# Loading the context in 2 KB pieces, chunk by chunk, beside transposes through DRAM

## The chip, the core and the metric

The kernel runs on one core of one Trainium2 chip. The time is that of the device for one launch, in microseconds (us); lower is better. The engines are TensorE (PE, with its weight loads PEld), VectorE (DVE), ScalarE (ACT), GpSimd (POOL) and SyncE (SP). ScalarE, SyncE and GpSimd also issue DMAs, each on a queue of its own.

## What is computed

One block of a perceiver on 16 items, all in float32: each item has 128 tokens of width 512 and a context of 2048 rows of width 512.

```python
# x: (16, 128, 512), ctx: (16, 2048, 512)
h = layernorm(x)
x = x + softmax(h @ ctx.T) @ ctx                       # cross attention on the context
h = layernorm(x)                                       # 16 heads, latent 64, head size 32
q, k, v = up(h @ Wq_down), up(h @ Wk_down), up(h @ Wv_down)   # half of q and k rotated
x = x + (softmax(causal(q @ k.T / sqrt(32))) @ v) @ Wc
h = layernorm(x)
gates = softmax_of_top2(h[:, 0] @ Wr.T)                # 2 of 8 experts, by the first token
x = x + h + sum_e gates[e] * (h @ A[e].T) @ Bw[e].T
```

## The kernel before

The work of an item `b` is cut into generators, which yield between parts: `score(b)` (first layernorm, scores against the context, softmax without its division), `attend(b)` (probabilities times context, division, residual, second layernorm), `inner(b)` (self attention, third layernorm) and `experts(b)` (gating, two gathered experts, result). A hand-written sequence of `step(kind, b)` calls (lines 985 to 1095) interleaves them, so that in turn `b` of the main loop (line 1050) `inner(b)`, `attend(b + 1)`, `score(b + 2)` and `experts(b - 1)` run together, and the layernorm of item `b + 3` as well. The last two items run in an order that is written out in `CLOSING` (line 48). Matmuls, TensorE transposes and loads keep the order of the program on their engine (`keep_in_program_order`, lines 136 to 145), and so do the instructions marked `pinned`.

The context comes from DRAM twice. `ctxT` is the context turned, laid out by the host for the scores; `load_turned` (line 339) brings it in four chunks of 1 MB, each 128 partitions by 4 by 512 numbers. `ctx` has the rows as they are, for `attend`; `load_ctx` (line 345) brings it in four chunks of 1 MB too. Both sets of tiles live in a pool of four buffers per name, so a chunk can be loaded once the same chunk of the item before has been used: a chunk of `ctxT` after its 16 score products (line 397), a chunk of `ctx` after its quarter of `attend` (line 459). In both loads each partition takes one piece of 8 KB: the host lays `ctxT` out so, and partition `p` takes rows `4p` to `4p + 3` of a chunk of `ctx`. From the main loop on both are issued on ScalarE's queue (`queue = nc.scalar`, line 1049): the four chunks of `ctx` of item `b + 2` after the third score bank is copied, the four of `ctxT` of item `b + 3` after the fourth bank and the copies of `yT` and `vv`. There they stand between the activations of that engine.

Activations are transposed in two steps. VectorE turns 32 by 32 blocks (into `blocks`, or `pX` for the probabilities of the self attention), and the blocks change place by a way through DRAM: `send` (line 224) writes them to a DRAM tile `there`, and `fetch` (line 232) reads them back, in pieces of 512 bytes into `hT` or of 1 KB into `pT`. These DMAs are all on SP's queue, and a fetch waits for its send to land. In each turn the two halves of the probabilities (`p_b_0`, `p_b_1`) and the second layernorm of item `b + 1` (`2_{b+1}`) go this way at the end of the self attention's softmax. TensorE uses `pT` in `y` (`weighted`, line 658) and the `hT` of item `b + 1` in `v` (`project`, line 528), after the score products of item `b + 2`, the expert's `mid` and its second product.

The softmax of `inner` is `weigh` (line 643), in four groups of four heads: mask, maximum, four exponentials on ScalarE, division, and the transposing of blocks. The chosen experts' weights are gathered by GpSimd (`each`, `wb`, lines 803 to 813).

Of the kernel before, what the change touches and what calls it, by code (L numbers as in the profile page):

```python
# [19 lines left out]
P = 128  # L20
B, S, V, D = 16, 128, 2048, 512
# [3 lines left out]
KC = D // P  # L25
VC = V // 512
# [15 lines left out]
MIX = [p % 4 * QD + p // 4 for p in range(P)]  # L42
# [47 lines left out]
def perceiver_block(ctx: ExitStack, tc: tile.TileContext, io: dict, out: bass.AP):  # L90
# [53 lines left out]
    def load(*args, queue=nc.sync):  # L144
        tc.keep_in_program_order(queue.dma_start(*args))

    queue = nc.sync
# [76 lines left out]
    def send(name):  # L224
        if name in ways:
            blocks, dst = ways[name]
            each = blocks.shape[2] * QD
            there = dram.tile([P, 4 * each], F32, tag=f"there_{each}", name=f"there_{name}")
            load(there, blocks.rearrange("p q n j -> p (q n j)"))
            ways[name] = there, dst  # L230

    def fetch(name):
        if name in ways:
            there, dst = ways.pop(name)
            load(
                dst.rearrange("p a n j -> p a (n j)"),
                there.rearrange("(a i) (q e) -> (i q) a e", a=4, q=4),
            )
# [94 lines left out]
    def load_x(b):  # L333
        xs[b] = p3.tile([P, D], F32, tag="x", name=f"x_{b}")
        load(xs[b], io["x"][b])
# [3 lines left out]
    def load_turned(b, vs=range(VC)):  # L339
        for v in vs:  # L340
            t = p4.tile([P, KC, 512], F32, tag="ctxT", name=f"ctxT_{b}_{v}")
            load(t, io["ctxT"][b, v], queue=queue)
            turned_cts.setdefault(b, []).append(t)

    def load_ctx(b, vs=range(VC)):
        for v in vs:
            t = p4.tile([P, 4, D], F32, tag="ctx", name=f"ctx_{b}_{v}")

            load(
                t, io["ctx"][b, v * 512 : (v + 1) * 512].rearrange("(p j) d -> p j d", j=4),  # L350
                queue=queue,
            )
            cts.setdefault(b, []).append(t)
# [621 lines left out]
    def step(kind, b, n=1):  # L975
        if not 0 <= b < B:
            return
        if (kind, b) not in gens:
            gens[kind, b] = kind(b)
        for _ in range(n):  # L980
            next(gens[kind, b])
# [11 lines left out]

    warm_up(15)
    load_turned(0, [0, 1])
    load_x(1)
    load_turned(0, [2, 3])
    load_ctx(0, [0])
    load_turned(1, [0, 1])
    load_ctx(0, [1])  # L1000
    load_turned(1, [2, 3])
    load_ctx(0, [2, 3])
    load(up, io["up"])
    step(score, 0, 2)
# [41 lines left out]
    step(inner, 0)  # L1046


    queue = nc.scalar
    for b in range(B - 2):  # L1050
        if b + 3 < B:
            load_x(b + 3)
        step(inner, b)
        step(experts, b - 1)
        send(f"3_{b - 1}")
        fetch(f"3_{b - 1}")
        if b:
            send(f"1_{b + 2}")
            fetch(f"1_{b + 2}")
        step(inner, b, 3)  # L1060
        step(score, b + 1, 2)
        step(attend, b + 1)
        step(inner, b)
        step(attend, b + 1)
        step(inner, b, 2)
        step(experts, b - 1)
        step(attend, b + 1)
        step(inner, b)
        step(attend, b + 1)
        step(experts, b - 1)  # L1070
        step(inner, b)
        step(experts, b - 1)
        step(inner, b + 1)
        send(f"p_{b}_0")
        fetch(f"p_{b}_0")
        send(f"p_{b}_1")
        send(f"2_{b + 1}")
        fetch(f"p_{b}_1")
        fetch(f"2_{b + 1}")
        step(score, b + 2, 2)  # L1080
        step(score, b + 3)
        step(score, b + 2)
        load_ctx(b + 2)
        step(score, b + 2)
        step(experts, b - 1)
        step(score, b + 2)
        step(experts, b - 1)
        step(inner, b)
        step(inner, b + 1)
        if b + 3 < B:  # L1090
            load_turned(b + 3)
        step(score, b + 2)
        step(score, b + 3)
        step(inner, b)
        step(score, b + 2)
# [63 lines left out]
```

## Time and profile before

| | us |
|---|---|
| median of 3 runs (810.36 to 811.34) | 810.94 |
| the profiled execution | 810.97 |
| its span | 809.2 |
| TensorE busy | 800.2 |
| VectorE busy | 529.7 |
| ScalarE busy | 260.4 |
| one turn of the main loop | 47.86 |

In the views, a line gives the engine, the line of the program, the operation, the tile written and those read, the shape and the count. `PEq`, `ACTq` and `SPq` are the sequencers of the engines, which issue DMAs. L137, L140, L115 and L145 are the helpers through which all instructions go, so groups are told apart by their tiles. The DMA engines' busy share is a mean over 16 engines; their queues are q10 (ScalarE's), q1 (SP's) and q0 (GpSimd's).

The matmuls of a turn keep the same order from turn to turn, and a turn of 47.86 us can be read from any pair of equal lines, such as the first product of `y` at 441.14 and at 489.00 us.

### The profile page before, as it was taken

What the parts mean: (1) busy time and instruction counts of PE and PEld (TensorE: products, weight loads), DVE (VectorE), ACT (ScalarE), POOL (GpSimd) and SP (SyncE); (2) the same over time, 40 slices, a digit from 0 to 9 for tenths busy, and PEclk for the clock granted to TensorE, in tenths of its full rate; (3) what the DMA queues carried; (4) which work ended last, traced back from release to release, by engine and by line L of the source; (5) the groups of instructions that cost most, each with busy time, mean ns of one, the idle gap of its engine ahead of it and who ended that gap; (6) DMA issues with size and microseconds to landing.
All of it is one profiled execution on the core that took longest, in us unless ns stands there. A gap on an engine that the chain in (4) does not pass through costs nothing.

```text
span 809.2 us, 14363 instructions
## 1 busy us (share of the span) xinstructions
PE 800.2 (99%) x5538; PEld 568.5 (70%) x5538; DVE 529.7 (65%) x1234; ACT 260.4 (32%) x772; POOL 146.6 (18%) x213
## 2 busy tenths in 40 slices
PE   9999999999999999999999999999999999999996
PEld 9946775768677576866758677676867757686653
DVE  2455759386684947658495775938667584856885
ACT  2232324142232423233241232415223241422461
POOL 1001011212121121211112121111212112121204
PEclk9999999999999999999999999999999999999999
DMA  9998394967849497694958859495885949664102
GB/s 375 417 389 321 118 380 171 340 253 251 360 163 381 172 324 292 221 397 142 364 212 292 320 188 399 152 353 222 281 337 181 388 152 340 261 231 173 41 1 79
DMA packets 76868, 211.05 MB, mean 261 GB/s; under 512 B 6400, under 2 KB 42624, under 8 KB 60416
## 3 DMA queue, kind: packets, MB, share of 16 engines
q10 hardware_dynamic: 15696, 113.32, 35.0%
q1 hardware_dynamic: 57168, 84.75, 29.4%
q0 software_dynamic: 3936, 12.07, 4.4%
q8 instruction: 44, 0.72, 0.3%
q14 instruction: 24, 0.20, 0.1%
HBM read 180.23 MB, written 29.88 MB: 260 GB/s over the span
## 4 chain that ended last, share of the span: by engine, by line
PE 97%; DVE 1%; POOL 0%; issue 0%; ACT 0%; POOLq 0%
PE psc L137 28%; PE av L137 28%; PE k L137 7%; PE q L137 7%; PE v L137 7%; PE o L137 6%; PE pss_sc L137 2%; PE y L137 2%; PE ffn L137 2%; PE pss_acc L137 2%; PE mid L137 2%; PE warm L137 1%; PE tr_m L140 0%; PE tr L140 0%; PE spread L137 0%; PE lg L137 0%
## 5 line engine op out<-in xcount | busy, mean ns | idle before, releaser
L137 PE MATMUL psc<-hT,ctxT 128*128 128x128 f32 x2048 | 235.0, 276 | 0.0
L137 PEld LDWEIGHTS psc<-hT,ctxT 128*128 128x128 f32 x2048 | 231.3, 192 | 0.5 <-issue 0.5
L137 PE MATMUL av<-ctx,sc 128*128 128x512 f32 x512 | 227.3, 596 | 0.0
L137 PEld LDWEIGHTS av<-ctx,sc 128*128 128x128 f32 x512 | 94.4, 190 | 110.5 <-issue 107.9
L115 ACT ACTIVATE att<-att,nmx 128x128 f32<-128x128 f32 x256 | 98.8, 388 | 84.9 <-DVE nmx L115 84.9
L115 POOL TENSOR_SCALAR rs<-mv 128x1 f32<-128x1 f32 x47 | 10.6, 225 | 431.0 <-DVE g_at L115 209.5
L115 ACT COPY sc<-psc 128x512 f32<-128x512 f32 x64 | 37.5, 586 | 140.0 <-PE psc L137 140.0
L115 ACT ACTIVATE sc<-sc 128x512 f32<-128x512 f32 x64 | 40.2, 630 | 90.9 <-DVE sc L115 90.4
L137 PE MATMUL k<-hT,w_k 128*128 128x128 f32 x512 | 60.1, 275 | 0.0
L137 PE MATMUL q<-hT,w_q 128*128 128x128 f32 x512 | 60.0, 275 | 0.0
L137 PEld LDWEIGHTS k<-hT,w_k 128*128 128x128 f32 x512 | 58.5, 192 | 1.5 <-issue 0.8
L137 PE MATMUL v<-w_v,hT 128*32 128x512 f32 x520 | 59.0, 593 | 0.0
L137 PEld LDWEIGHTS q<-hT,w_q 128*128 128x128 f32 x512 | 58.5, 192 | 0.0
L137 PE MATMUL o<-w_c,yT 128*128 128x512 f32 x128 | 57.8, 594 | 0.0
L115 DVE TENSOR_TENSOR mx<-psc,mx 128x512 f32<-128x512 f32 x32 | 21.6, 676 | 55.0 <-ACT sc L115 55.0
L115 ACT ACTIVATE kb<-kT,cst 128x512 f32<-128x512 f32 (+1 forms) x34 | 36.2, 1113 | 39.8 <-DVE kT L115 39.8
L115 DVE TENSOR_SCALAR h<-x,mv,rs 128x512 f32<-128x512 f32 x47 | 27.4, 583 | 31.9 <-POOL rs L115 31.9
L115 ACT ACTIVATION_READ_ACCUMULATOR att<-att,nmx 128x1 f32 x256 | 47.9, 187 | 0.0
L115 DVE TENSOR_TENSOR sc<-sc,spread 128x512 f32<-128x512 f32 x64 | 42.6, 671 | 3.3 <-PE spread L137 3.3
L115 DVE TENSOR_TENSOR att<-att,rsm 128x512 f32<-128x512 f32 x64 | 43.4, 678 | 0.8
L115 DVE TENSOR_REDUCE nmx<-att 128x4 f32<-128x512 f32 x64 | 41.8, 671 | 0.1
L137 PEld LDWEIGHTS o<-w_c,yT 128*128 128x128 f32 x128 | 23.9, 196 | 23.8 <-issue 23.0
(139 smaller groups left out, 851.1 us busy)
## 6 DMA issues: line engine op xcount, KB each, us to landing
ctx<-in_ctx_dram ACTq DMA_DIRECT2D x56, 1024.0 KB, 8.4
ctxT<-in_ctxT_dram ACTq DMA_DIRECT2D x52, 1024.0 KB, 10.5
there_p<-pX SPq DMA_DIRECT2D x28, 512.0 KB, 4.0
pT<-there_p SPq DMA_DIRECT2D x28, 512.0 KB, 4.5
ctxT<-in_ctxT_dram SPq DMA_DIRECT2D x12, 1024.0 KB, 8.9
there<-blocks SPq DMA_DIRECT2D x42, 256.0 KB, 3.3
hT<-there SPq DMA_DIRECT2D x42, 256.0 KB, 3.0
ctx<-in_ctx_dram SPq DMA_DIRECT2D x8, 1024.0 KB, 10.5
```

The source lines that it names most:

```text
L115: ins = issue(*args, **kwargs)
L137: tc.keep_in_program_order(nc.tensor.matmul(*args, **kwargs))
```

## The change

A load of a chunk is made of pieces of 2 KB instead of 8 KB. For `ctxT` the host lays the four parts of a chunk one after the other, each 128 partitions by 2 KB; for `ctx` partition `p` takes rows `p`, `p + 128`, `p + 256` and `p + 384` of the chunk. The order of rows in the scores follows from this in the same way.

The loads are no longer issued four at a time. A chunk of `ctx` is issued after the second, third and fourth group of the self attention's exponentials and after the copy of the first score bank; `ctxT` follows chunk by chunk after the second and third bank and with two chunks after the fourth. The order of the matmuls does not change. The loads before the main loop keep their places.

```diff
     def load_turned(b, vs=range(VC)):
         for v in vs:
             t = p4.tile([P, KC, 512], F32, tag="ctxT", name=f"ctxT_{b}_{v}")
-            load(t, io["ctxT"][b, v], queue=queue)
+            load(t, io["ctxT"][b, v].rearrange("c p n -> p c n"), queue=queue)
...
             load(
-                t, io["ctx"][b, v * 512 : (v + 1) * 512].rearrange("(p j) d -> p j d", j=4),
+                t, io["ctx"][b, v * 512 : (v + 1) * 512].rearrange("(j p) d -> p j d", p=P),
                 queue=queue,
             )
...
         step(attend, b + 1)
         step(inner, b, 2)
+        load_ctx(b + 2, [0])
         step(experts, b - 1)
         step(attend, b + 1)
         step(inner, b)
+        load_ctx(b + 2, [1])
         step(attend, b + 1)
         step(experts, b - 1)
         step(inner, b)
+        load_ctx(b + 2, [2])
         step(experts, b - 1)
         step(inner, b + 1)
         send(f"p_{b}_0")
...
         fetch(f"p_{b}_1")
         fetch(f"2_{b + 1}")
-        step(score, b + 2, 2)
+        step(score, b + 2)
+        load_ctx(b + 2, [3])
+        step(score, b + 2)
+        if b + 3 < B:
+            load_turned(b + 3, [0])
         step(score, b + 3)
         step(score, b + 2)
-        load_ctx(b + 2)
+        if b + 3 < B:
+            load_turned(b + 3, [1])
         step(score, b + 2)
         step(experts, b - 1)
         step(score, b + 2)
+        if b + 3 < B:
+            load_turned(b + 3, [2, 3])
         step(experts, b - 1)
         step(inner, b)
         step(inner, b + 1)
-        if b + 3 < B:
-            load_turned(b + 3)
         step(score, b + 2)
...
         "ctxT": laid(
-            p["ctx_1024"].reshape(B, VC, P, 4, KC, P)[..., MIX].transpose(0, 1, 5, 4, 3, 2)
-        ).reshape(B, VC, P, KC, 512),
+            p["ctx_1024"].reshape(B, VC, 512, KC, P)[..., MIX].transpose(0, 1, 3, 4, 2)
+        ),
```

## The prediction

> **What bounds the kernel now.** I read the page's busy times first, then the chain that ended last, then one turn of the loop in order of time, then the DMA landings, and last the DMA share by stretch.
>
> ```profile
> PE 800.2 (99%) x5538; PEld 568.5 (70%) x5538; DVE 529.7 (65%) x1234; ACT 260.4 (32%) x772; POOL 146.6 (18%) x213
> PE 97%; DVE 1%; POOL 0%; issue 0%; ACT 0%; POOLq 0%
> q10 hardware_dynamic: 15696, 113.32, 35.0%
> q1 hardware_dynamic: 57168, 84.75, 29.4%
> q0 software_dynamic: 3936, 12.07, 4.4%
> ```
>
> TensorE is busy for 800.2 of 809.2 us and makes 97% of the chain. The three DMA queues together fill 69% of the 16 engines: DMA is no bound on average, but it is no idle resource either. Of the 9.0 us that TensorE idles, 1.0 lies ahead of the first matmul and nearly all the rest after 760 us, in the closing order, which the change leaves alone. So there is almost nothing to win, and the question is whether TensorE's order, which it keeps, is made to wait.
>
> One turn of the loop takes 47.86 us. The timeline of TensorE around the end of a turn (start, duration, what):
>
> ```profile
> 462.01 10.57 PE L137 MATMUL av<-ctx,sc 128*128 128x512 f32 x24
> 486.26 1.06 PE L137 MATMUL mid<-hT,wa 128*128 128x128 f32 x8
> 489.00 1.08 PE L137 MATMUL y<-pT,vv 128*32 128x128 f32 x32
> 489.89 2.33 PE L137 MATMUL v<-w_v,hT 128*32 128x512 f32 x20
> ```
>
> And the DMA issues on SP's and ScalarE's queues, the last two lines from the turn before:
>
> ```profile
> 470.53 0.32 SPq L145 DMA_DIRECT2D there_p<-pX  x1
> 473.15 0.37 SPq L145 DMA_DIRECT2D pT<-there_p  x1
> 473.61 0.46 SPq L145 DMA_DIRECT2D there_p<-pX  x1
> 477.82 0.32 SPq L145 DMA_DIRECT2D there<-blocks  x1
> 478.89 0.37 SPq L145 DMA_DIRECT2D pT<-there_p  x1
> 480.55 0.37 SPq L145 DMA_DIRECT2D hT<-there  x1
> 435.98 1.96 ACTq L145 DMA_DIRECT2D ctx<-in_ctx_dram  x4
> 445.80 1.90 ACTq L145 DMA_DIRECT2D ctxT<-in_ctxT_dram  x4
> ```
>
> The transposes through DRAM run from 470.5 on. The second pT landed 4.0 us after its issue, at 482.9, and y needs it at 489.0; hT landed 3.8 us after its issue, at 484.35, and v needs it at 489.89. Over the turns from 138 us on, hT lands 3.4 to 5.5 us ahead of v (some 4.8 on average, 2.9 in the first turn) and pT 3.8 to 6.1 us ahead of y. **These few microseconds are all the cover there is.** The context loads stay out of the way now: ctx is issued at 435.98 + 47.86 = 483.8, when the transposes are all but over, and ctxT at 493.7.
>
> How full the DMA engines are there (stretch, engine columns empty, granted clock, DMA share, GB/s):
>
> ```profile
> 472.00:473.00 1.00, 1.00 0.59 238
> 476.00:477.00 1.00, 1.00 1.08 386
> 482.00:483.00 1.00, 1.00 1.06 372
> DMA packets 1027, 2.04 MB, mean 408 GB/s; under 512 B 32, under 2 KB 32, under 8 KB 1027
> DMA packets 294, 2.12 MB, mean 424 GB/s; under 512 B 35, under 2 KB 35, under 8 KB 35
> ```
>
> The shares from 470 to 484 add up to 9.9 us of all 16 engines. The last two lines are 5 us each of saturated loads: 36 to 41 us, the k weight in pieces of 2 KB (line 287), and 54 to 59, ctxT in pieces of 8 KB. They price the smaller piece: 4% less rate, so 2.57 against 2.47 us a megabyte-load, and 1027/16/5 = 12.8 packets per engine and us, 78 ns each.
>
> [...] The trace is compatible with either size of a turn: a there<-blocks of 256 KB issued at 455.98 beside 8 KB ctxT loads took 4.9 us, against 2.2 to 2.7 away from them; its 8 packets per engine behind 8 packets of 0.31 us are 2.5 us, and that is also one whole load. [...]
>
> **The change part by part.**
>
> *Pieces of 2 KB.* The 64 ctxT and 64 ctx loads go from 128 packets to 512. That adds 0.10 us each, 0.8 us of DMA a turn, hidden by the 31% of free DMA time. Only the head is saturated (share 1.0 from 3 to 75 us). The load with the least room there is ctxT chunk 0 of context 1: it lands at 21.2 and TensorE takes it up at about 22.3. Some 6.8 MB precede it, so it comes 0.7 us later: still in time. I take 0; the bounds are 0 and, if the head ran at the 340 GB/s of some stretches of weight loading at 43 to 48 us, +4.
>
> *Eight DMA issues moved on ScalarE's queue.* They cost 0.34 to 0.56 us each (median 0.41), before and after. Three now stand among the 16 exponentials of 0.385 us that run back to back from 464.7 to 471.0: after the 8th, the 12th and the last. Behind the first two wait groups 2 and 3, and behind these VectorE's scaling and transposes to pX. The second there_p would be ready up to 0.8 us later, but it stands in SP's queue behind the first pT, which lands only at 477.4: hidden. Each ctx issue waits for TensorE to be done with its buffer: quarter 0 of av at 460, quarter 1 at 465.5, quarter 2 at 469.0; the issues fall at some 468.1, 470.0 and 471.8, so none waits. The others come just after the copy of a score bank whose matmuls freed the buffer.
>
> *Completion semaphores.* The 19 hardware DMAs of a turn share eight of these in turn, so each issue waits for the eighth before it. ctx chunk 3 (at 477.3) thus waits for chunk 1, and ctxT chunk 0 (480.7) for ctx chunk 2. Behind the second on ScalarE is the copy of score bank 2, due at 483.8. I put chunk 2's landing at 482 to 483: 1 us of cover, cost 0; if it is gone, the running maximum is late, not TensorE's next matmul. SP's present wait for ctx (98.3 us in 13 turns) goes; it ends before VectorE's blocks are ready, so nothing is gained.
>
> *Loads beside transposes.* This decides. From 468.1 to 489.9, 21.8 us, ScalarE's queue now holds ctx 0 to 3 and ctxT 0 and 1: six loads, 15.0 us at 2.5. With the 9.9 us of transposes and gathers that is 24.9 us of work in 21.8: **3.1 us too much**, so ScalarE's queue is backlogged nearly throughout. From the first there_p to hT, SP's queue has per engine 8 + 32 + 8 + 8 + 32 + 32 = 120 packets. If each lets one 2 KB packet pass, 120 x 78 ns = 9.4 us are added; less the 4.8 us of cover, v waits 4.6 us. That is the upper bound for turns by packet. The lower is 0, if the gaps in SP's chain let ScalarE's queue run dry or SP's packets are hardly held up. The excess of 3.1 us would be the wait if hT were served last; a part falls on ctxT chunk 1. I take 2.7 us a turn. The gathers (3.5 us to landing, wa ready at 481.9 for mid at 486.26) get some 4 us later, inside the same wait.
>
> A wait at v shifts the whole next turn, as attend, softmax and loads all follow from it, so it comes again: 13 turns (contexts 0 to 12; the 14th loads no ctxT) x 2.7 = 35 us.
>
> *Sum.* Span 809.2 + 35 = 844.2; with 810.97 - 809.2 = 1.8 around it, 846. The profiled execution's 810.97 stands 0.03 above the median of 810.94, so the same holds for that.
>
> **The rivals.** A is the forecast.
>
> B, no change: the cover holds. Place: hT ahead of v. Price 0, and the head's 0.7 us hidden: 811. It decides as long as less than 4.8 us are added, that is, if fewer than 62 of the 120 packets have to let one pass. For it: DMA has 31% free over the turn, SP's chain has long gaps, and small reads mixed with large ones reached 386 GB/s. Against it: 24.9 us of work in 21.8.
>
> C, much slower: a turn is a whole load, not a 2 KB packet. Then there_p, there, both pT and hT each wait up to 2.5 us; five of these are 12.5, less 4.8 is 7.7; with some gaps 6.5. 13 x 6.5 = 85: 895.
>
> D, faster: the loads' removal from 483 to 505 would have to shorten head or tail. TensorE idles 9.0 us in all, and I find no DMA that releases those waits in the tail: at most 1 us, 810, and below 809.3 only by something I don't see.
>
> E, the head alone stalls (2 KB pieces at 340 GB/s), the turns do not: +4, 815.
>
> **How the numbers follow.** About 0.2% (1.6 us) is what a measurement of this kernel can tell from no change. Chances: A 0.56, with its own range from 1.4 to 4.5 us a turn, 829 to 869; B 0.20; C 0.13; D 0.04; E 0.07. Slower: A, C and E, 0.76; same: B, 0.20; faster: D, 0.04. The range from 809.5 to 869 holds A, B and E and leaves out C and D, 0.17.
>
> **What would show it.** Right: between 130 and 730 us turns of about 50.6 us instead of 47.86; TensorE waiting at v (or y) for hT (or pT); hT at 7 to 9 us to landing in that place and pT at 6 to 7; DMA share near 1.0 from 470 to 500. Wrong: turns still 47.86 long with hT landing ahead of v (B); pT and there_p at 9 us and more (C); TensorE waiting for ctxT before 50 us (E); copies of the score banks late behind ScalarE's DMA issues, with mx the last to come, which I priced at nothing.

## The result and the profile after

| | before | after |
|---|---|---|
| median, us | 810.65 (4 runs, 810.17 to 811.34) | 998.49 (4 runs, 997.6 to 1002.77) |
| span of the profiled execution, us | 809.2 | 996.0 |
| TensorE busy, us | 800.2 | 840.7 |
| TensorE idle, us | 9.0 | 155.3 |
| one turn, us | 47.86 | 61.9 in the median (58.6 to 64.6) |

The ratio is 1.2327 (95% interval 1.2289 to 1.2364). The kernel became 188 us slower where 35 were forecast. In the experiments below, three of the four runs of the kernel with two early chunks, the profiled one among them, were slow ones (860.46 to 869.35, the fourth 847.45), so it has no ratio. From the page of the changed kernel, the busy times, the chain that ended last, and the queues:

```profile
PE 840.7 (84%) x5538; PEld 577.2 (58%) x5538; DVE 536.3 (54%) x1234; ACT 260.7 (26%) x772; POOL 150.8 (15%) x213
...
q10 hardware_dynamic: 57168, 113.32, 32.3%
q1 hardware_dynamic: 64848, 84.75, 23.7%
q0 software_dynamic: 3936, 12.07, 4.1%
...
DMA 39%; PE 30%; DVE 21%; POOL 4%; issue 3%; SPq 2%; ACT 0%; DVEq 0%; ACTq 0%; POOLq 0%
```

The chain was 97% TensorE. Now DMA leads it, although the queues move the same bytes as before and are busy for 60% of a longer span: it is latency, not volume. TensorE's waits (total in us, times, longest):

```profile
PE y L137 <- DMA pT<-there_p: 110.8, 19, 9.2
PE v L137 <- DMA hT<-there: 32.6, 13, 3.3
PE ffn L137 <- ACT mid L115: 2.6, 2, 2.2
```

The difference of the spans, 186.8 us, is 146.3 us more idle time, nearly all in these two waits, and 40.5 us more busy time of the same 5538 matmuls. The group of `v` shows where most of the latter comes from: 821 ns each, against 593 before, 27.1 us in all.

```profile
L137 PE MATMUL v<-w_v,hT 128*32 128x512 f32 x520 | 86.1, 821 | 32.6 <-DMA hT<-there 32.6
```

One turn on SP's queue and on ScalarE's, and TensorE at its end:

```profile
517.68 0.32 SPq L145 DMA_DIRECT2D there_p<-pX  x1
525.23 0.37 SPq L145 DMA_DIRECT2D pT<-there_p  x1
525.69 1.19 SPq L145 DMA_DIRECT2D there_p<-pX  x1
526.93 0.42 SPq L145 DMA_DIRECT2D there<-blocks  x1
538.00 0.37 SPq L145 DMA_DIRECT2D pT<-there_p  x1
539.29 0.37 SPq L145 DMA_DIRECT2D hT<-there  x1
```

```profile
512.86 0.38 ACTq L145 DMA_DIRECT2D ctx<-in_ctx_dram  x1
514.45 0.37 ACTq L145 DMA_DIRECT2D ctx<-in_ctx_dram  x1
515.95 0.37 ACTq L145 DMA_DIRECT2D ctx<-in_ctx_dram  x1
...
523.41 0.37 ACTq L145 DMA_DIRECT2D ctx<-in_ctx_dram  x1
...
527.07 0.37 ACTq L145 DMA_DIRECT2D ctxT<-in_ctxT_dram  x1
```

```profile
536.02 0.64 PE L137 MATMUL y<-pT,vv 128*32 128x128 f32 x16 [0.18 <-DMA pT<-there_p]
544.90 1.08 PE L137 MATMUL y<-pT,vv 128*32 128x128 f32 x16 [8.24 <-DMA pT<-there_p]
549.24 4.92 PE L137 MATMUL v<-w_v,hT 128*32 128x512 f32 x32 [3.26 <-DMA hT<-there]
```

A fetch is issued as soon as its send has landed (in the kernel before, the last update of the first send's semaphore stands at 473.09 us and its fetch at 473.15). From issue to issue the first send takes 7.55 us (2.62 before), the second 12.31 (5.28). hT then takes 9.95 us to `v` (3.8 to its landing before) and is issued 1.29 us behind the second fetch (1.66 before). The four differences, 4.9 + 7.0 + 6.15 - 0.4, make 17.7 us, of which the cover takes 5.5 (484.35 to 489.89 in the turn before). So `v` starts 12.2 us later after the first send than before; with the slower products this turn is 13.5 us longer.

What the queues move tells how. From 518 to 519 us, just after the send was issued (packets, MB, share of 16 engines):

```profile
DMA packets 158, 0.32 MB, mean 324 GB/s; under 512 B 0, under 2 KB 0, under 8 KB 158
...
q10 hardware_dynamic: 158, 0.32, 98.0%
```

SP's queue, q1, has no line: not one packet of the send has moved. q1's first packets come at 521.9, 4.2 us after the issue; before, 0.8 us after it. The reverse holds from 530 to 531, when the first fetch runs and a ctxT load that was issued at 527.07 is not moving yet (the six packets of q10 end the ctx load ahead of it; from 530.5 to 531.2 q10 has none, and q1 122):

```profile
q1 hardware_dynamic: 227, 0.23, 78.0%
q0 software_dynamic: 21, 0.07, 33.8%
q10 hardware_dynamic: 6, 0.01, 2.7%
```

From 545 to 546 both have long been under way, the fetch of hT in pieces of 512 bytes and the load in pieces of 2 KB:

```profile
q10 hardware_dynamic: 162, 0.32, 81.8%
q1 hardware_dynamic: 155, 0.08, 26.2%
```

About one packet for one packet, as the forecast assumed; from 533 to 534 it is 102 to 103, and from 522 to 523, just behind the send's start, 96 to 55. These are counts over 16 engines, some ten for each engine and queue, so they do not tell in what order one engine took the packets of the two. What the forecast lacked is the late start.

It stood in the profile of the kernel before. The there<-blocks issued at 455.98 beside ctxT loads, which the prediction read as 4.9 us and put down to turns of either size, moved nothing in its first two microseconds, while the loads filled the engines. From 457 to 458:

```profile
q10 hardware_dynamic: 53, 0.42, 98.6%
```

### The profile page after: what moved, and what is told of

Its sections match the earlier page's. It is cut to its first block, busy times and chain, and to the rows that moved or that the text cites. A ratio compares the mean times of both kernels' runs of the same rounds, so it can differ in the third digit from the quotient of the medians.

```text
span 996.0 us, 14350 instructions
## 1 busy us (share of the span) xinstructions
PE 840.7 (84%) x5538; PEld 577.2 (58%) x5538; DVE 536.3 (54%) x1234; ACT 260.7 (26%) x772; POOL 150.8 (15%) x213
## 4 chain that ended last, share of the span: by engine, by line
DMA 39%; PE 30%; DVE 21%; POOL 4%; issue 3%; SPq 2%; ACT 0%; DVEq 0%; ACTq 0%; POOLq 0%
DMA there<-blocks 14%; DMA hT<-there 13%; DMA there_p<-pX 10%; PE v L137 9%; PE o L137 6%; DVE att L115 5%; PE av L137 4%; PE psc L137 4%; DVE sums L115 3%; DVE nmx L115 2%; DVE sc L115 2%; SPq L145 2%; POOL qP L115 2%; DVE pX L115 2%; POOL kP L115 2%
## 5 line engine op out<-in xcount | busy, mean ns | idle before, releaser
L115 DVE TENSOR_REDUCE nm<-tr_m 128x1 f32<-128x128 f32 x16 | 4.7, 292 | 227.2 <-PE tr_m L140 227.2
L137 PE MATMUL y<-pT,vv 128*32 128x128 f32 x512 | 27.0, 345 | 110.9 <-DMA pT<-there_p 110.8
L137 PE MATMUL v<-w_v,hT 128*32 128x512 f32 x520 | 86.1, 821 | 32.6 <-DMA hT<-there 32.6
L115 POOL TENSOR_SCALAR rs<-mv 128x1 f32<-128x1 f32 x47 | 10.6, 225 | 615.6 <-DVE mv L115 372.5
L137 PEld LDWEIGHTS y<-pT,vv 128*32 128x32 f32 x512 | 15.4, 132 | 126.3 <-DMA pT<-there_p 122.2
L137 PEld LDWEIGHTS v<-w_v,hT 128*32 128x32 f32 x520 | 21.5, 145 | 88.2 <-issue 85.6
L115 ACT ACTIVATE kb<-kT,cst 128x512 f32<-128x512 f32 (+1 forms) x34 | 36.2, 1113 | 39.7 <-DVE kT L115 39.7
L115 ACT COPY yT<-y 128x512 f32<-128x512 f32 (+1 forms) x17 | 9.5, 561 | 141.0 <-PE y L137 98.1
```

Source lines behind the costliest of these rows:

```text
L115: ins = issue(*args, **kwargs)
L137: tc.keep_in_program_order(nc.tensor.matmul(*args, **kwargs))
```

## The experiments

The theories, assumptions that the runs were to test, by the numbers in the quoted expectations: 1, turns go by packet, so larger pieces make the sends wait longer; 2, a turn is a whole DMA; 3, the small pieces themselves are the harm; 4, DMAs of both queues are taken into service in the order of their issue, about two of a queue at a time, and share by packet from then on; 5, formed on the way: what SP issues starts only when what was issued before it on the other queue is (nearly) through. "Send 1" is the first `there_p`, "send 2" the second, "send 3" the `there` of the layernorm; the table gives the median of 14 turns from the issue of a send to that of its fetch.

| kernel | time, us | ratio (95% interval) | send 1 | send 2 | send 3 |
|---|---|---|---|---|---|
| before | 810.65 | 1 | 2.6 | 5.3 | 2.4 |
| after | 998.49 | 1.2327 (1.2289 to 1.2364) | 8.2 | 11.6 | 11.9 |
| places of after, 8 KB | 1006.67 | 1.2373 (1.2298 to 1.2449) | 7.9 | 13.4 | 13.2 |
| places of before, 2 KB | 811.24 | 1.0009 (1.0000 to 1.0018) | 2.6 | 5.4 | 2.3 |
| only ctx moved | 881.14 | 1.0867 (1.0813 to 1.0920) | 7.7 | 9.5 | 9.3 |
| only ctxT moved | 877.66 | 1.0827 (1.0742 to 1.0912) | 2.6 | 5.5 | 2.7 |
| each load as two DMAs | 961.88 | 1.1862 (1.1839 to 1.1886) | 7.6 | 10.8 | 10.6 |
| two ctx chunks early | 860.95 | | 5.9 | 4.0 | 4.9 |
| three ctx chunks early | 865.75 | 1.0677 (1.0656 to 1.0699) | 7.9 | 6.2 | 6.9 |
| three ahead of send 1 | 881.79 | 1.0875 (1.0805 to 1.0946) | 8.1 | 7.1 | 7.3 |
| one beside send 3 | 893.52 | 1.1007 (1.0987 to 1.1028) | 2.6 | 5.5 | 7.4 |
| loads on GpSimd's queue | 823.78 | 1.0162 (1.0142 to 1.0183) | 2.6 | 5.4 | 2.4 |
| busy wait at y | 1004.31 | 1.2398 (1.2377 to 1.2418) | 8.0 | 11.9 | 12.2 |
| busy wait at y and v | 990.85 | 1.2222 (1.2201 to 1.2242) | 7.9 | 11.2 | 11.9 |
| a quarter of each load | 811.90 | 1.0016 (1.0006 to 1.0026) | 2.6 | 5.3 | 3.1 |
| half of each load | 817.48 | 1.0078 (1.0055 to 1.0101) | 4.1 | 5.4 | 5.3 |

### Pieces or places

The places of the changed kernel with the old pieces (and the old layout of ctxT by the host), and, with the same lines the other way round in the kernel before, the old places with the new pieces:

```diff
 # places of after, 8 KB
-            load(t, io["ctxT"][b, v].rearrange("c p n -> p c n"), queue=queue)
+            load(t, io["ctxT"][b, v], queue=queue)
...
-                t, io["ctx"][b, v * 512 : (v + 1) * 512].rearrange("(j p) d -> p j d", p=P),
+                t, io["ctx"][b, v * 512 : (v + 1) * 512].rearrange("(p j) d -> p j d", j=4),
```

> The changed kernel with the old pieces of 8 KB; only the places of the loads are new. Theory 1 (the DMA engines take turns by packet, as forecast): every packet of SP's queue now lets a packet of 0.31 us pass instead of 0.08, so the transposes come later than in the changed kernel, over 1050 us. Theory 2 (turns go by whole loads of 1 MB): the same as the changed kernel or 1% better by the rate of the pieces, 985 to 1000. Theory 3 (the packets of both queues are made and taken in the order of issue, and a load of 512 packets fills that line where one of 128 does not): SP's DMAs are let through, under 900.

> The kernel before with pieces of 2 KB; the loads keep their old places. Theories 1 and 2: the transposes are out of the way of the loads as before, 811 to 813. Theory 3: the transposes that stand beside the end of the ctxT loads (third and first layernorm) come later, but they have over 20 us of cover; 811 to 820.

The pieces do next to nothing at either place: 1006.67 against 998.49 (the four runs with 8 KB go from 995.43 to 1007.49), and 811.24 against 810.5 in the same comparison. Theories 1 and 3 fall; theory 2 had put 1000 as its upper end. With 8 KB pieces too, q1 moves nothing for 4.0 us (issue at 526.04, first packet at 530.1), and once both are under way packets of 8 KB and of 1 KB come about one for one, here from 552 to 553 us:

```profile
q10 hardware_dynamic: 47, 0.34, 83.2%
q1 hardware_dynamic: 51, 0.05, 15.8%
```

### Which of the moved loads

In each of these kernels one context keeps the order of before, four chunks issued together.

```diff
 # only ctx moved: the three load_turned of after out, and as before
         step(inner, b + 1)
+        if b + 3 < B:
+            load_turned(b + 3)
         step(score, b + 2)
...
 # only ctxT moved: the four load_ctx of after out, and as before
         if b + 3 < B:
             load_turned(b + 3, [1])
+        load_ctx(b + 2)
         step(score, b + 2)
```

> The changed kernel with ctxT issued in its old place, four chunks together; only the four chunks of ctx are new in place, in 2 KB pieces. Theories 2 and 3: three to four loads instead of six stand before the transposes, so roughly half of the loss goes, 880 to 930. Theory 1: four loads of 10 us of DMA fit into the window with the 9.9 us of transposes, 811 to 830.

> The changed kernel with ctx issued in its old place after the third score bank, four chunks together; only ctxT is moved, chunk by chunk after the second, third and fourth bank. Theory 4: there_p and the first pT go undisturbed; the second pT and hT meet two ctxT chunks and then ctx, so a part of the loss is there, 830 to 900. If the loss of the changed kernel were the early ctx chunks alone, 811 to 820.

The losses are alike, 71 and 67 us, but not their causes. With ctx moved TensorE waits 39.7 us for pT. With ctxT moved the transposes are as fast as before, and the mid activation is late:

```profile
PE ffn L137 <- ACT mid L115: 41.4, 13, 4.4
```

ScalarE stands at its own DMA issues. Its timeline in one turn:

```profile
421.88 0.37 ACTq L145 DMA_DIRECT2D ctxT<-in_ctxT_dram  x1
422.35 6.23 ACTq L145 DMA_DIRECT2D ctx<-in_ctx_dram  x4
428.68 0.37 ACT L115 ACTIVATE mid<-mid,g_gate 128x128 f32<-128x128 f32 x1 [6.28 <-DMA ctxT<-in_ctxT_dram]
```

Four issues take 6.23 us, not 1.9, and behind them stands the activation that `ffn` needs. The last two of them take most of it:

```profile
423.98 1.94 ACTq L145 DMA_DIRECT2D ctx<-in_ctx_dram  x1
425.95 2.62 ACTq L145 DMA_DIRECT2D ctx<-in_ctx_dram  x1
```

The completion semaphores that these two wait for (in the kernel before, that of the pT issued at 478.89 has its last update at 482.88, when pT had landed) had their last updates at 417.8 and 421.0 us, so it is not they that hold them; no issue of this kernel starts just behind such an update. Four loads were under way at each, and each issue ended about when the oldest was through (425.9 and 428.6; the last packets of those loads end at 426.0 and 428.4). What held them, no run shows. The prediction put the cost of ScalarE's issues at zero. For the changed kernel that is right (2.6 us of waiting for mid in all), for this order it is not.

### Two DMAs for a load

```diff
-            load(t, io["ctxT"][b, v].rearrange("c p n -> p c n"), queue=queue)
+            for h in (0, 2):
+                load(
+                    t[:, h : h + 2], io["ctxT"][b, v, h : h + 2].rearrange("c p n -> p c n"),
+                    queue=queue,
+                )
 # and ctx likewise
```

> The changed kernel with every chunk loaded by two DMAs of 512 KB, in 2 KB pieces as there. Theory 2: a turn of ScalarE's queue is half as long, so the waits of SP's DMAs shrink by about half, 890 to 930. Theories 1 and 3: bytes, packets and their order are the same, so no change, 985 to 1010, unless ScalarE is held up by the more frequent waits for completion semaphores.

The sends take 0.6 to 1.3 us less, not half. The turn as a whole DMA, theory 2, is not what sets the delay. The time is confounded: TensorE waits 40.6 us for mid here, as ScalarE has twice the issues and here they do wait for completion semaphores: 42 of them come just behind the last update of the semaphore that they share with an earlier DMA, as one at 520.34 behind the second there_p (issued at 509.94, last update at 520.32).

### How many loads ahead, and how long ahead

```diff
 # two early: ctx 0 and 1 at the places of after, the rest as before
+        load_ctx(b + 2, [0])
...
+        load_ctx(b + 2, [1])
...
-        load_ctx(b + 2)
+        load_ctx(b + 2, [2, 3])
 # three early: ctx 0, 1, 2 so, and [3] at the old place
 # three ahead of send 1: [0, 1, 2] together, after the last group's exponentials
 # one beside send 3: [0] after the first score bank, [1, 2, 3] at the old place
```

> The changed kernel with only chunks 0 and 1 of ctx in their new places; chunks 2 and 3 and ctxT are issued where the kernel before issues them, all in pieces of 2 KB. Theory 2 (turns of whole loads): the first there_p moves no packet until each engine is through with chunk 1, then has the engines alone. Theory 4 (turns by packet once a DMA is in service, but DMAs of both queues are taken into service in the order of their issue, about two of a queue at a time): it starts within 1.5 us of its issue and mixes with chunk 1, packet by packet. Both: what comes after it is undisturbed, 811 to 820.

> Chunks 0 to 2 of ctx in their new places, chunk 3 and ctxT in the old ones, pieces of 2 KB. When the first there_p is issued some 2.0 MB of the three loads are outstanding. Theory 5 (an SP DMA moves only when nearly all that was issued before it on the other queue is through, in order of issue): there_p takes 8 us to the issue of its fetch, 2.6 more than with two chunks (5.9). Theory 2 (it waits for the one load that is being moved): the same 5.9 as with two. Time 860 to 885.

> The same three chunks, all issued together after the last exponentials of the softmax, just ahead of the first there_p, so that nearly all of 3 MB is outstanding at its issue. Theory 5: there_p takes 9.5 to 11 us to the issue of its fetch. Theory 2: it waits for chunk 0 alone, 4 to 5.5 us. Theory 1 (turns by packet at once): 3.3 us. Time by theory 5: 870 to 900; by theory 1: 811 to 830.

> One load alone is put beside the transposes: chunk 0 of ctx after the first score bank; chunks 1 to 3 and ctxT stay in the old places, pieces of 2 KB. All theories: the second there_p or pT is later by up to 2.6 us, the 4.8 us ahead of v hold, and the time is that of the kernel before, 811 to 814. If even one load costs over 1%, the cover in front of v and y is smaller than the forecast had it.

Send 1 takes 5.9 us with two loads ahead of it and 7.9 with three, when these are issued 1.5 us apart; 8.1 with three that are issued together, less than the 9.5 that theory 5 gave as its least (a turn that I followed in the trace has 9.4). In that turn the first packets of the send come at 408.7, when 1.4 MB of the three loads have moved, the second is under way and the third has not begun: theory 5 as it was put, all that was issued before, is too strong. Two early chunks were expected to cost at most 10 us by both theories and cost 37 to 59; theory 4, by which send 1 starts within 1.5 us there, falls, as it took 2.4. One load beside send 3 was expected to cost nothing and cost 83 us. The single load shows how one delay leads to the next. SP, ScalarE and TensorE in one turn:

```profile
411.83 0.32 SPq L145 DMA_DIRECT2D there<-blocks  x1
413.01 0.37 SPq L145 DMA_DIRECT2D pT<-there_p  x1
419.21 0.37 SPq L145 DMA_DIRECT2D hT<-there  x1
```

```profile
410.64 0.37 ACTq L145 DMA_DIRECT2D ctx<-in_ctx_dram  x1
...
417.84 1.52 ACTq L145 DMA_DIRECT2D ctx<-in_ctx_dram  x3
```

```profile
429.46 3.29 PE L137 MATMUL v<-w_v,hT 128*32 128x512 f32 x13 [5.39 <-DMA hT<-there]
```

Send 3 is issued 1.19 us after the load and moves nothing until 415.9, when the load is nearly through (its last packets end at 417.05). So the fetch of hT is issued at 419.21, which is 1.37 us *after* the three other loads instead of 3.3 us ahead of them (480.55 and 483.84 in the kernel before). It moves its first packets at 423.5, when the first of the three is through, and then shares with the others. A slip of 5 us in send 3 has turned hT's landing from 3.8 into 10 us, and `v` waits. That a DMA starts late behind the other queue, theory 5 says, but I had not followed it past the first send.

### Bytes or DMAs

Every issue stays where the changed kernel has it, but each load of the main loop brings a part of its chunk only; the rest of the tile keeps an earlier item's numbers.

```diff
-            load(t, io["ctxT"][b, v].rearrange("c p n -> p c n"), queue=queue)
+            n = 1 if queue is nc.scalar else KC
...
+            load(t[:, :n], io["ctxT"][b, v, :n].rearrange("c p n -> p c n"), queue=queue)
 # ctx likewise; n = 2 for half
```

> The changed kernel with all its DMA issues at their places, but in the main loop each load brings only the first quarter of its chunk (256 KB, 128 pieces of 2 KB); the rest of the buffer keeps what an earlier item left there. Theory 5 (a send waits for the bytes that were issued before it on the other queue): a quarter load is through in about 0.65 us and the loads are issued 1.5 us apart, so nothing is outstanding when a send is issued: sends of the first probabilities take 2.6 to 3.2 us to the issue of their fetch, the turn is 47.9 us, 811 to 825. Rival (each DMA ahead costs a fixed time, whatever its size, be it by its issue, its semaphore or a switch of queues): about 8 us as in the changed kernel, turns near 60, 960 to 1000.

> As the kernel with quarters, but each load brings the first half of its chunk (512 KB, 256 pieces of 2 KB). Theory 5: a half load is through in about 1.3 us, just under the 1.5 us between two issues, so at most one is outstanding at a send: 3 to 4 us for the first send, turn 48 to 51, 811 to 850. Rival (fixed time for each DMA): as with quarters, 960 to 1000. A cost in proportion to bytes alone, without a threshold, would give half of the loss: about 905.

This is the clearest pair. With the same DMAs at the same places, a quarter of the bytes costs 1.3 us and half costs 6.9, where a whole costs 188. It is no cost per DMA, and the time is not in proportion to bytes either: **it has a threshold.** The threshold is the cover. With half loads the sends are late already, send 1 by 1.5 us and send 3 by 2.9 in the median, but that still fits ahead of `v`, and TensorE waits for hT 2.5 us in all. With whole loads it no longer fits. Loads of 1 MB come every 1.5 us, 0.7 MB/us, and the DMA engines drain 0.3 to 0.4; those of 0.5 MB bring 0.34. With half loads the send was issued at 473.55 with some 0.7 MB outstanding, against 2.0 in the changed kernel. From 474 to 475:

```profile
q10 hardware_dynamic: 205, 0.40, 103.4%
q1 hardware_dynamic: 2, 0.01, 2.0%
```

and from 475 to 476, when the load runs out:

```profile
q1 hardware_dynamic: 80, 0.33, 79.5%
q10 hardware_dynamic: 64, 0.10, 27.0%
```

It started 1.4 us after its issue. By the same count (bytes of the loads issued, less what q10 had moved by then), 1.0 MB outstanding went with 2.4 us (two early), 2.0 MB with 4.2 us (after) and 2.9 MB with 4.9 us (three ahead of send 1): in these turns some 2 us for each MB at first, less at the end. Another count fits these turns better. From the issue of the last load ahead of it, the send's first packets come after 5.7 us (two early), 5.9 (after), 5.6 (three ahead of send 1) and 5.3 (send 3 behind one load), whatever is outstanding, and after 3.2 with half loads; the fetch of hT behind three loads came after 4.6. No run was made to tell the two counts apart.

### Another queue for the loads

```diff
-    queue = nc.scalar
+    queue = nc.gpsimd
```

> The changed kernel with its loads of the main loop on GpSimd's queue instead of ScalarE's; the gathers stand in the same queue. Theory 4: that queue has an intake of its own, so SP's DMAs start within 1.5 us of their issue beside the loads and lose only by packets; TensorE's waits for pT and hT fall under 60 us together; 840 to 920, as the gathers may come later. Theory 2: SP's DMAs wait for whole loads as before, 960 to 1010.

The sends are as fast as before, and 823.78 is below both ranges (840 to 920, 960 to 1010), but this doesn't test the theories: on GpSimd's queue the loads are issued elsewhere (ctx chunks 0 and 1 at 426.4 and 432.0, well ahead of the send at 436.5, the next ones from 449.1, when the transposes are nearly over). It shows that loads kept out of the transposes' way leave the turn at 47.9 us; one turn alone lost 11.

### The slower matmuls

Dummy products, overwritten later, keep TensorE busy while it would wait: 20 ahead of the second half of `y`, then 34 there and 14 ahead of `v`.

```diff
                 first = c // 2 * 8 + c % 2 * 2
+                if c == 2 and b < B - 2:
+                    for _ in range(20):
+                        matmul(acc[:, c * P : (c + 1) * P], ones, ones, start=True, stop=True)
```

> The changed kernel with 20 more products of a constant by itself (4.5 us) before the second half of y in the main loop, where TensorE waits some 8 us for pT; they write columns that the half overwrites. If the lower granted clock after that wait is a part of the loss, v runs at 0.6 us a product instead of 0.8 and the time falls by 10 to 30 us, 968 to 988. If only the arrival of pT and hT counts, 996 to 1003; if the products are late themselves, more.

> The changed kernel with products of a constant in both waits of TensorE: 34 ahead of the second half of y (some 7.6 us) and 14 ahead of v (3.1 us), so that it stands idle little and the granted clock should stay high through v. If the low clock of v counts, the time falls by 1.2 to 2 us a turn, 970 to 985; if the arrival of pT and hT alone counts, 996 to 1005.

The first left the wait at `v`, after which `v`'s products still took 805 ns, and told nothing. The second removed the low clock: 0.997 on the mean instead of 0.912, `v`'s products at 592 ns. It brought 7.6 us, between its two ranges. This is a least value, as the dummy products ended after hT was there in all but two turns (TensorE waits for it twice, 0.8 us). That the rest of the 40.5 us of added busy time lay where TensorE would have waited otherwise is likely, but no run shows it.

## Why the prediction was wrong, step by step

*Pieces of 2 KB, cost 0.* Right: 0.7 us at the old places. Rival E, a stalled head, did not occur: TensorE never waits for ctxT in the changed kernel.

*Eight issues on ScalarE's queue, cost 0.* Right in cost: the exponentials still follow each other by 0.385 us. Wrong in time: I put the first three issues 2.4 us ahead of the first send at the earliest. They are 4.8 us ahead, as an issue comes some five exponentials before its place among them (at 512.86 behind three of the 16 exponentials, where the program has eight). That brought more backlog ahead of the send.

*Completion semaphores, cost 0.* Right for the changed kernel, and wrong as a rule: with each load as two DMAs they hold ScalarE, and TensorE waits 40.6 us for mid. In the kernel before, eight are shared in turn: the loads issued at 493.66 to 495.11 have those of the DMAs issued at 477.82 to 480.97, the eighth before each. In the changed kernel ctxT chunk 0 (527.07) has that of the first send (517.68), not that of ctx chunk 2. The 41 us with ctxT alone moved are another hold-up of the same issues, which the prediction did not have.

*Loads beside transposes, 2.7 us a turn.* **This step failed.** Its form was that each packet on SP's queue lets one 2 KB packet pass, 9.4 us at most. That was an assumption of mine. Once both are moving, the counts are about as it has them (162 packets to 155 from 545 to 546 us); the order on one engine is not shown. But a DMA that was just issued does not take part at once: the first send starts 1.4 to 4.9 us after its issue where loads stand ahead of it on the other queue, 0.8 where none do, and the transposes are a chain of DMAs in which one after the other meets such a backlog. The delay ahead of `v` was 17.7 us, not the 7.5 that the forecast amounts to with its 4.8 of cover.

*The rate in that sum.* 2.5 us a load (2.57 by its own reading for 2 KB) was too good as well: from 514 to 520 the loads, alone, moved 1.81 MB, 0.30 MB/us, which is 3.5 us a load. Six of them are 20.8 us; with the 9.9 of the transposes that is 30.7 us of work in 21.8, so 8.9 too much, not 3.1. Why the rate is 302 GB/s there and 408 elsewhere is open.

*13 turns x the wait.* Right: 13 turns of some 14 us are 182 of the 187.

*Rivals.* B, the cover holds, is refuted. It decided "as long as fewer than 62 of 120 packets let one pass"; the late start of the first send alone, 4.9 us in the turn shown, used nearly all of it. C, a whole load ahead of each DMA, foresaw there_p and pT at 9 us and more. This was seen for the second there_p (12.3 us to the issue of its fetch) and the first pT (10.8 us to `y`), but as a mechanism it is refuted by the halves and by the send that starts in the middle of a load (408.7, with three issued together), and its 895 us were short too. D did not occur.

*The clock.* Not in the prediction. In this turn TensorE waits from 536.66 to 544.90 us, and the trace has the granted clock at 0.50 from 541.6 to 551.9, at 1.00 before and after. The stretch from 545 to 546 us (column 7 is the granted clock):

```profile
545.00:546.00 1.00, 0.98 (x16) 0.50 (x16) 0.00 (x0) 0.00 (x0) 0.00 (x0) 0.50 1.08 397
```

It is worth at least 7.6 us of the 188.

What stays open is what holds a newly issued DMA back. In the changed kernel the send starts with some 0.8 MB of the 2.0 still to move, so it is not a strict order of issue over the whole core. Whether it is one on each of the 16 engines is not shown, as the profile gives the mean over the engines alone. With three loads issued together the median was 8.1 us where a strict order asks for 9.5 or more, and the near constant time from the last load's issue is unexplained. Sends and loads on one queue were not tried.

## What to carry to other kernels

Loads that fill idle DMA time were free here only as long as their backlog was nearly drained whenever a short DMA with a waiting reader was issued, or its delay fitted the cover: compare their bytes per microsecond between two issues with what the engines drain (here 0.3 to 0.4 MB/us), not their sum with the average share. Price a chain of dependent DMAs per link, each at the backlog that it meets (here a start 2.4 to 4.9 us after the issue behind loads of 1 MB, 1.4 behind loads of 0.5), look in the profile at hand for a link that already meets one, and check whether a late link falls behind the next burst of loads. Where TensorE is 99% busy, as before the change, there is next to nothing to win, and the order of before is to be kept: none of the kernels tried beats it.

## What was not expected of the hardware

- A DMA issued on one queue, with 0.7, 1.0, 2.0 and 2.9 MB outstanding on another, moved its first packets after 1.4, 2.4, 4.2 and 4.9 us, against 0.8 with none. A load behind transposes started late too (issued at 527.07, first packets at 531.3, 0.8 us after its own queue had run empty).
- In the stretches shown with two queues under way, both moved about as many packets, with unlike sizes of packets: 162 to 155 with 2 KB and 512 bytes, 47 to 51 with 8 KB and 1 KB.
- ScalarE issued DMAs some five exponentials ahead of their place, but where issues were held up with four loads of 1 MB under way (6.23 us for four issues), the activation behind them waited too.
